# Every steady-state product of a two-layer graph kernel issued as two 64-column tiles of the TensorE array

## The chip, the cores and the metric

The kernel runs on one core of one Trainium2 chip. The metric is the device time of one execution in microseconds. Before the change it is 2427.78 us, the median of 6 runs (2426.64 to 2429.95).

## The reference

There are 128 graphs of 128 nodes with 512 features, and each has a 0/1 adjacency matrix. Layer 0 is graph attention with 8 heads of 64 features; layer 1 is a hypergraph convolution to 1024 features, a layer norm, and a second convolution back to 512. Each layer has a residual and a layer norm. Everything is fp32.

```python
# layer 0
feats = einsum('bnf,hfu->bhnu', X, W)                 # 512 -> 8 x 64
dense = leaky_relu(e_self[..., :, None] + e_neigh[..., None, :])
att = softmax(dense - 1e10 * (1 - A), axis=-1)
x = layernorm(x + relu(einsum('bhij,bhju->bhiu', att, feats) + b))
# layer 1
def hypergraph_conv(x, adj, W, b):
    H = (adj != 0); w = adj[:, 0, :]                   # weights: first row
    m = Be * einsum('nce,nch->neh', H, x @ W.T)        # Be = 1 / sum over nodes
    return Dn * einsum('nce,neh->nch', H, m) + b       # Dn = 1 / (H w)
h = layer_norm(relu(hypergraph_conv(x, adj, W1, b1)))  # 512 -> 1024
x = layernorm(x + hypergraph_conv(h, adj, W2, b2) + x) # 1024 -> 512
```

## The kernel before, in words

The graphs are taken in 64 pairs. All steps of a pair are functions that are recorded with a lag (in pairs) and a time; the list of all steps of all pairs is sorted by that time once, and in this order the instructions are given out (`todo`, at the end of the kernel). So each engine has one fixed order, in which up to five pairs are interleaved. The distance of two pairs in that order is `T = 38.6` units; only the order matters on the chip.

TensorE (PE) does per pair, with names of the PSUM tiles as the profile has them:

- `pz` (L808): the propagation of layer 0's output, 8 products of 128 stationary by 128 moving columns;
- `pd` (L435): the pair's propagator, 2 products of 128 by 128;
- `phX`, `phY`, `phW` (L843): the hidden convolution, 7 block products of 8 matmuls each, 128 by 128. The blocks are those of a seven-product (Strassen-like) scheme, with sums made by GpSimd and VectorE;
- `pq` (L1009): the last propagation, 2 products with 512 moving columns;
- `pfX`, `pfY`, `pfW` (L479, `rows_product`): layer 0's features, 7 block products of 2 matmuls each with 264 moving columns;
- `pyX`, `pyY`, `pyW` (L479 too): the second weights, 7 block products of 4 matmuls each with 257 or 256 moving columns;
- `pav` (L696, `attend_pair`): attention, 16 heads times two halves of the output rows.

The seven products accumulate in three banks, X, Y and W. ScalarE copies X after the first two of X's products (`copy`, L335) while PE is in the product between, and PE's next product into X waits for that copy.

`pav` alone is already given as column tiles: it writes output partitions 0 to 63 and 64 to 127 with two matmuls, each with 64 stationary columns and 65 moving ones. All other products have 128 stationary columns, the array's full width.

An fp32 matmul of the program becomes two pairs of a weight load (LDWEIGHTS) and a matmul (MATMUL) on PE; the profile counts those. The first two pairs and the last one have steps of their own (`plain_features` L516, `last_weigh` L1055, `last_output` L1091, transposes by PE in L388, L644, L976, L1062).

Of the kernel before, what the change touches and what calls it, by code (L numbers as in the profile page):

```python
# [20 lines left out]
def kernel(  # L21
# [45 lines left out]
    nc = tc.nc  # L67
    G, N, F = x.shape
    P = 128
# [3 lines left out]
    KF = F // P  # L73
    KH = DH // P
    HALF = 512
    QU = HALF // 2
# [12 lines left out]
    def bank(name):  # L89
        return psum.tile([P, HALF], F32, tag="bank", name=name)  # L90


    st = [{} for _ in range(PAIRS)]

# [212 lines left out]
    def step(lag, time, since=0, until=PAIRS):  # L307

        def keep(fn):
            steps.append((lag, time, fn.__name__, range(since, until), fn, ()))  # L310
            return fn
        return keep
# [117 lines left out]
    @step(1, 40.1)  # L430
    def propagator(p, s):

        s["pd"] = bank(f"pd_{p}")
        for g in range(2):
            nc.tensor.matmul(  # L435
                s["pd"][:, g * N:(g + 1) * N], s["hB"][:, g, :], s["hT"][:, g, :],
                start=True, stop=True,
            )

    @step(1, 40.2)  # L440
# [22 lines left out]
    def halves(t, n):  # L463
        return [[t[:, g, :n], t[:, g, n:]] for g in range(2)]
# [7 lines left out]
    def rows_product(s, i, a, sums, w, n, nk, extra, to, start):  # L472

        lhs = {1: a[0][0], 2: a[0][1], 3: sums[:, 3], 4: a[1][1], 5: sums[:, 0], 6: sums[:, 1],
               7: sums[:, 2]}[i]
        rhs = w[:, {1: 0, 2: 1, 3: 2, 4: 3, 5: 4, 6: 5, 7: 6}[i]]
        n += extra if i in (1, 2, 6) else 0
        for k in range(nk):
            nc.tensor.matmul(  # L479
                to[:, :n], lhs[:, k, :], rhs[:, k, :n], start=bool(start) and k == 0,  # L480
                stop=(k == nk - 1), skip_group_check=True,
            )

    FW = HH * UW
# [1 line left out]
    def feature(s, i, to, start):  # L486
        rows_product(s, i, halves(s["xT"], KF // 2), s["xS"],
                     w0_sb.rearrange("p b k h u -> p b k (h u)"), FW, KF // 2, 0, to, start)
# [316 lines left out]
    def propagate(p, s, g):  # L805
        t = s["pz", g] = bank(f"pz_{p}_{g}")
        for k in range(KF):
            nc.tensor.matmul(  # L808
                t[:, k * N:(k + 1) * N], s["y"][:, g, k * P:(k + 1) * P], s["R"][:, g, :],
                start=True, stop=True,  # L810
            )

    at(3, 0.0, propagate, 0)
    at(3, 0.9, propagate, 1)

    def z_evict(p, s, g):
# [19 lines left out]
    def hidden(s, i, to, start):  # L836
        w = w1_sb[:, {1: 0, 2: 1, 3: 6, 4: 2, 5: 3, 6: 4, 7: 5}[i]]
        b, t = halves(s["zT"], KF // 2), s["zS"]
        rhs = {1: b[0][0], 2: b[0][1], 3: b[1][1], 4: t[:, 3], 5: t[:, 0], 6: t[:, 1],
               7: t[:, 2]}[i]  # L840
        for m in range(KH // 2):
            for k in range(KF // 2):
                nc.tensor.matmul(  # L843
                    to[:, m * N:(m + 1) * N], w[:, k, m * P:(m + 1) * P], rhs[:, k, :],
                    start=bool(start) and m == 0 and k == 0, stop=(k == KF // 2 - 1),
                    skip_group_check=True,
                )

    chain("ph", 3, (2.0, 3.8, 5.6, 7.35, 9.1, 12.65, 14.4, 4.0, 5.95, 11.0), hidden,
          HALF)  # L850

# [60 lines left out]
    def weigh(s, i, to, start):  # L912
        rows_product(s, i, halves(s["h"], KH // 2), s["hS"], w2_sb, QU, KH // 2, 1, to, start)

    chain("py", 3, (21.0, 29.4, 27.7, 32.9, 31.2, 35.35, 37.1, 23.0, 29.6, 33.1), weigh,
          QU, 1, until=LAST)
# [89 lines left out]

    def output(p, s, g):
        s["pq", g] = bank(f"pq_{p}_{g}")
        nc.tensor.matmul(  # L1009
            s["pq", g], s["R"][:, g, :], s["y2"][:, g, :, :QU], start=True, stop=True  # L1010
        )

    at(4, 10.9, output, 0, until=LAST)
    at(4, 11.8, output, 1, until=LAST)

    def o_sum(p, s, g):
# [31 lines left out]
    def last_weigh(p, s, g, j, some=(0, 1)):  # L1048
        if some[0] == 0:
            s["py", g, j] = bank(f"py_{g}{j}")  # L1050
        t = s["py", g, j]
        n = QU + (j == 0)
        for i in some:
            for k in range(KH // 2):
                nc.tensor.matmul(  # L1055
                    t[:, :n], s["h"][:, g, i * KH // 2 + k, :], s["w2"][i][j][:, k, :n],
                    start=(i == 0 and k == 0), stop=(i == 1 and k == KH // 2 - 1),
                )

    def last_sum_squares(p, s, g):  # L1060
# [27 lines left out]
    def last_output(p, s, g, j):  # L1088
        if j == 0:
            s["pq", g] = bank(f"pq_{g}")  # L1090
        nc.tensor.matmul(  # L1091
            s["pq", g][:, j * QU:(j + 1) * QU], s["R"][:, g, :], s["y2"][:, g, j, :QU],
            start=True, stop=True,
        )

    def last_o_sum(p, s, g, j):
# [21 lines left out]
    for t, fn, *args in (  # L1118
        (8.0, last_weights),
        (24.2, last_weigh, 0, 0), (27.8, last_weigh, 0, 1), (31.3, last_sum_squares, 0),  # L1120
        (31.4, last_h_rstd, 0), (31.5, last_weigh, 1, 0), (32.5, last_scale, 0, 0),
        (32.6, last_scale, 0, 1), (34.9, last_sum_squares, 1), (35.0, last_h_rstd, 1),
        (35.1, last_output, 0, 0), (35.2, last_output, 0, 1), (35.3, last_weigh, 1, 1, (0,)),
        (35.5, last_o_sum, 0, 0), (35.6, last_scale, 1, 0), (36.0, last_o_sum, 0, 1),
        (36.5, last_o_rstd, 0), (37.0, last_output, 1, 0), (37.1, last_weigh, 1, 1, (1,)),
        (37.2, last_o_sum, 1, 0), (38.7, last_scale, 1, 1), (38.75, last_norm, 0),
        (38.9, last_output, 1, 1), (39.6, last_o_sum, 1, 1), (40.0, last_o_rstd, 1),
        (40.5, last_norm, 1),
    ):
        at(3, t, fn, *args, since=LAST)  # L1130
# [135 lines left out]
```

## Time and profile before

| what | value |
|---|---|
| median of 6 runs | 2427.78 us |
| the profiled execution's own time | 2427.62 us |
| its span, first to last instruction | 2425.8 us |
| mean granted TensorE clock | 0.997 |
| PE busy, share of the span | 2397.0 us, 99% |
| VectorE (DVE) / GpSimd (POOL) / ScalarE (ACT) busy | 80% / 74% / 63% |
| LDWEIGHTS and MATMUL on PE | 18273 of each |
| time from one pair to the next in the steady state | 37.05 us |

The busy times are unions of the instructions' recorded spans, and a matmul's recorded span reaches past the next one's start. So the mean of one (275 ns at 128 columns) is not what it costs; the distance from start to start is.

### The profile page before, as it was taken

What the parts mean: (1) busy time and instruction counts of PE and PEld (TensorE: products, weight loads), DVE (VectorE), ACT (ScalarE), POOL (GpSimd) and SP (SyncE); (2) the same over time, 40 slices, a digit from 0 to 9 for tenths busy, and PEclk for the clock granted to TensorE, in tenths of its full rate; (3) what the DMA queues carried; (4) which work ended last, traced back from release to release, by engine and by line L of the source; (5) the groups of instructions that cost most, each with busy time, mean ns of one, the idle gap of its engine ahead of it and who ended that gap; (6) DMA issues with size and microseconds to landing.
All of it is one profiled execution on the core that took longest, in us unless ns stands there. A gap on an engine that the chain in (4) does not pass through costs nothing.

```text
span 2425.8 us, 52771 instructions
## 1 busy us (share of the span) xinstructions
PE 2397.0 (99%) x18273; PEld 2139.6 (88%) x18273; DVE 1946.6 (80%) x4456; ACT 1516.8 (63%) x4481; POOL 1793.7 (74%) x2060
## 2 busy tenths in 40 slices
PE   7999999999999999999999999999999999999998
PEld 5888998998988988989989889889899898898897
DVE  7888878878878888888788788888887887888876
ACT  4665765756756657657567566576575675665763
POOL 5777777777777777777777777777777777777774
PEclk9999999999999999999999999999999999999999
DMA  6555545545455455454454554554545545545531
GB/s 186 140 140 153 146 132 151 146 135 151 141 144 148 140 153 145 133 154 142 137 147 148 141 148 142 151 147 132 155 143 134 153 141 146 145 140 153 147 111 53
DMA packets 432762, 345.30 MB, mean 142 GB/s; under 512 B 153176, under 2 KB 382064, under 8 KB 432496
## 3 DMA queue, kind: packets, MB, share of 16 engines
q1 hardware_dynamic: 429024, 337.46, 48.9%
q10 hardware_dynamic: 3472, 4.47, 0.6%
q8 instruction: 145, 2.38, 0.4%
q14 instruction: 121, 0.99, 0.2%
HBM read 239.08 MB, written 102.73 MB: 141 GB/s over the span
## 4 chain that ended last, share of the span: by engine, by line
PE 95%; DMA 2%; DVE 1%; POOL 1%; ACT 1%; issue 0%; SPq 0%; ACTq 0%; POOLq 0%; DVEq 0%
PE pyX L479 18%; PE phX L843 18%; PE pfX L479 9%; PE phW L843 9%; PE pyW L479 9%; PE pav L696 5%; PE pz L808 5%; PE pfW L479 5%; PE phY L843 4%; PE pyY L479 4%; PE pq L1009 4%; PE pfY L479 2%; PE pd L435 1%; DMA w<-in_w1t_dram 0%; PE py L1055 0%
## 5 line engine op out<-in xcount | busy, mean ns | idle before, releaser
L335 ACT COPY py<-pyX 128x257 f32<-128x257 f32 x189 | 70.9, 375 | 531.3 <-PE pyX L479 531.3
L843 PEld LDWEIGHTS phX<-zS,w_sb 128*128 128x128 f32 x3072 | 362.9, 192 | 34.3 <-issue 29.9
L843 PE MATMUL phX<-zS,w_sb 128*128 128x128 f32 x3072 | 374.5, 275 | 3.1 <-POOL xS L461 2.5
L896 POOL TENSOR_TENSOR sq<-sq 128x512 f32<-128x512 f32 (+2 forms) x384 | 323.3, 842 | 20.2
L582 POOL TENSOR_TENSOR nb<-nb,neg 128x512 f32<-128x512 f32 x256 | 318.2, 1276 | 7.8 <-DMA nb<-rd 7.8
L598 ACT ACTIVATE nb<-nb,ft 128x128 f32<-128x128 f32 x1020 | 318.0, 391 | 7.5 <-POOL nb L582 7.5
L758 POOL TENSOR_TENSOR rso<-veo,mhalf 128x2 f32<-128x2 f32 x63 | 44.1, 700 | 372.3 <-DVE veo L756 372.3
L612 ACT ACTIVATE nb<-nb,nm 128x128 f32<-128x128 f32 x1024 | 312.9, 391 | 2.0 <-DVE nm L604 1.9
L604 DVE TENSOR_REDUCE nm<-nb 128x4 f32<-128x512 f32 x256 | 172.6, 682 | 136.5 <-ACT nb L598 122.3
L873 ACT ACTIVATE h<-h,vecs 128x128 f32<-128x128 f32 x768 | 245.1, 392 | 46.5 <-DVE h L858 46.5
L479 PE MATMUL pyX<-w_sb,hS 128*128 128x257 f32 x1008 | 245.6, 385 | 0.0
L479 PE MATMUL pyX<-w_sb,h 128*128 128x257 f32 x1008 | 239.3, 379 | 0.5 <-ACT py L335 0.5
L479 PE MATMUL pyW<-w_sb,hS 128*128 128x256 f32 x1008 | 238.7, 379 | 1.0 <-DVE y L927 1.0
L479 PEld LDWEIGHTS pyX<-w_sb,h 128*128 128x128 f32 x1008 | 190.9, 190 | 29.0 <-ACT py L335 0.9
L479 PEld LDWEIGHTS pyW<-w_sb,hS 128*128 128x128 f32 x1008 | 190.6, 189 | 29.0 <-issue 1.4
L479 PEld LDWEIGHTS pyX<-w_sb,hS 128*128 128x128 f32 x1008 | 185.7, 189 | 28.7
L999 DVE SCALAR_TENSOR_TENSOR y<-y,rsh,bw_bc 128x512 f32<-128x512 f32 x126 | 148.0, 1213 | 32.6 <-POOL rsh L995 32.4
L633 DVE STREAM_TRANSPOSE eT<-eb 128x512 f32<-128x512 f32 x252 | 163.6, 687 | 1.1 <-DMA eb<-ed 1.1
L502 DVE TENSOR_TENSOR ft<-pf,pfW 128x264 f32<-128x264 f32 x124 | 53.3, 429 | 135.6 <-PE pfW L479 88.9
L884 ACT ACTIVATE sq<-h 128x512 f32<-128x512 f32 x256 | 160.5, 628 | 2.1
L461 POOL TENSOR_TENSOR hS<-h 128x512 f32<-128x512 f32 x126 | 159.0, 1282 | 1.9 <-ACT h L873 1.9
L733 POOL TENSOR_TENSOR y<-y,b_bc 128x512 f32<-128x512 f32 x128 | 160.0, 1271 | 0.0
(178 smaller groups left out, 5693.6 us busy)
## 6 DMA issues: line engine op xcount, KB each, us to landing
nb<-rd SPq DMA_DIRECT2D x127, 512.0 KB
ed<-nb SPq DMA_DIRECT2D x126, 512.0 KB
eb<-ed SPq DMA_DIRECT2D x504, 128.0 KB
x<-in_x_dram SPq DMA_DIRECT2D x64, 512.0 KB
out_dram<-o SPq DMA_DIRECT2D x63, 512.0 KB
xb<-in_x_dram SPq DMA_DIRECT2D x248, 128.0 KB
a<-in_adj_dram SPq DMA_DIRECT2D x64, 128.0 KB
w<-in_adj_dram SPq DMA_DIRECT2D x128, 64.0 KB
```

The source lines that it names most:

```text
L461: engine.tensor_tensor(t[:, i], in0, in1, op=op)
L479: nc.tensor.matmul(to[:, :n], lhs[:, k, :], rhs[:, k, :n], start=bool(start) and k == 0, stop=(k == nk - 1), skip_group_check=True,)
L582: nc.gpsimd.tensor_tensor(t, t, neg[:, :, None, :].to_broadcast([P, NB, HH, B]), op=ALU.add)
L598: nc.scalar.activation(t, t, AF.Prelu, bias=s["ft"][:, g, h, 0:1], alpha=SLOPE)
L604: nc.vector.tensor_reduce(s["nm"][:, g, hs], scores(p, s, g, hs).rearrange("p b h j -> p h b j"), AX.XY, ALU.max, negate=True,)
L612: nc.scalar.activation(t, t, AF.Exp, bias=s["nm"][:, g, h:h + 1])
L633: nc.vector.transpose(s["eT"][:, g, hs, :].rearrange("p h (b i) -> p h b i", b=NB), s["eb", g][:, :, hs, :].rearrange("p b h j -> p h b j"),)
L733: nc.gpsimd.tensor_tensor(s["y"][:, g, :], s["y"][:, g, :], b0_bc, op=ALU.add)
L843: nc.tensor.matmul(to[:, m * N:(m + 1) * N], w[:, k, m * P:(m + 1) * P], rhs[:, k, :], start=bool(start) and m == 0 and k == 0, stop=(k == ...
L873: nc.scalar.activation(dst[:, k, :], src[:, k, :], AF.Relu, bias=b1_sb[:, c:c + 1])
L884: nc.scalar.activation(s["sq"][:, g, q * KH // 2:(q + 1) * KH // 2, :], hid(s, g, q), AF.Square, scale=DH ** -0.5,)
L896: nc.gpsimd.tensor_tensor(t[:, :n, :], t[:, :n, :], t[:, n:2 * n, :], op=ALU.add)
```

## The change

A helper `columns` is added. It gives a product as two matmuls, one for the stationary columns 0 to 63 (output partitions 0 to 63) and one for columns 64 to 127 (output partitions 64 to 127), each with all the moving columns. The matmuls of `propagator`, `rows_product`, `propagate`, `hidden`, `output`, `last_weigh` and `last_output` go through it. `attend_pair` and `attend` were in this form already. `plain_features`, `prepare_output`, `prepare_output_spread` and the transposes are left with 128 columns.

```diff
+    def columns(to, lhs, rhs, start, stop):
+
+        for c in range(2):
+            rows = slice(c * P // 2, (c + 1) * P // 2)
+            nc.tensor.matmul(
+                to[rows], lhs[:, rows], rhs, start=start, stop=stop, skip_group_check=True
+            )
...
         for g in range(2):
-            nc.tensor.matmul(
-                s["pd"][:, g * N:(g + 1) * N], s["hB"][:, g, :], s["hT"][:, g, :],
-                start=True, stop=True,
+            columns(
+                s["pd"][:, g * N:(g + 1) * N], s["hB"][:, g, :], s["hT"][:, g, :], True, True
             )
...
         for k in range(nk):
-            nc.tensor.matmul(
-                to[:, :n], lhs[:, k, :], rhs[:, k, :n], start=bool(start) and k == 0,
-                stop=(k == nk - 1), skip_group_check=True,
+            columns(
+                to[:, :n], lhs[:, k, :], rhs[:, k, :n], bool(start) and k == 0, k == nk - 1
             )
...
         for k in range(KF):
-            nc.tensor.matmul(
+            columns(
                 t[:, k * N:(k + 1) * N], s["y"][:, g, k * P:(k + 1) * P], s["R"][:, g, :],
-                start=True, stop=True,
+                True, True,
             )
...
             for k in range(KF // 2):
-                nc.tensor.matmul(
+                columns(
                     to[:, m * N:(m + 1) * N], w[:, k, m * P:(m + 1) * P], rhs[:, k, :],
-                    start=bool(start) and m == 0 and k == 0, stop=(k == KF // 2 - 1),
-                    skip_group_check=True,
+                    bool(start) and m == 0 and k == 0, k == KF // 2 - 1,
                 )
...
-        nc.tensor.matmul(
-            s["pq", g], s["R"][:, g, :], s["y2"][:, g, :, :QU], start=True, stop=True
-        )
+        columns(s["pq", g], s["R"][:, g, :], s["y2"][:, g, :, :QU], True, True)
...
             for k in range(KH // 2):
-                nc.tensor.matmul(
+                columns(
                     t[:, :n], s["h"][:, g, i * KH // 2 + k, :], s["w2"][i][j][:, k, :n],
-                    start=(i == 0 and k == 0), stop=(i == 1 and k == KH // 2 - 1),
+                    i == 0 and k == 0, i == 1 and k == KH // 2 - 1,
                 )
...
-        nc.tensor.matmul(
-            s["pq", g][:, j * QU:(j + 1) * QU], s["R"][:, g, :], s["y2"][:, g, j, :QU],
-            start=True, stop=True,
+        columns(
+            s["pq", g][:, j * QU:(j + 1) * QU], s["R"][:, g, :], s["y2"][:, g, j, :QU], True, True
         )
```

## The prediction

> **What bounds the kernel now.** I read the busy table first, then the chain that ended last, then PE's waits, and last PE's order of time over one pair.
>
> ```profile
> span 2425.8 us, 52771 instructions
> PE 2397.0 (99%) x18273; PEld 2139.6 (88%) x18273; DVE 1946.6 (80%) x4456; ACT 1516.8 (63%) x4481; POOL 1793.7 (74%) x2060
> PE 95%; DMA 2%; DVE 1%; POOL 1%; ACT 1%; issue 0%; SPq 0%; ACTq 0%; POOLq 0%; DVEq 0%
> ```
>
> ```profile
> PE px L388 <- DMA x<-in_x_dram: 9.5, 1, 9.5
> PE pz L808 <- ACT y L785: 6.8, 1, 6.8
> PE phX L843 <- POOL xS L461: 2.5, 1, 2.5
> PE pyW L479 <- DVE y L927: 1.0, 1, 1.0
> ```
>
> PE is 99% busy and carries 95% of the chain. Its waits for others sum to some 23 us, single ones, all in the first 90 us or the last pair. In the 62 steady pairs PE waits for nobody, so the change is worth what it makes of PE's own stream. This is one stretch of it, in order of time:
>
> ```profile
> 1112.39 1.05 PE L479 MATMUL pfX<-w_sb,xS 128*128 128x264 f32 x4
> ...
> 1117.69 1.05 PE L479 MATMUL pfW<-w_sb,xS 128*128 128x264 f32 x4
> 1118.67 2.09 PE L696 MATMUL pav<-ft,eT 128*64 128x65 f32 x64
> 1120.69 2.01 PE L479 MATMUL pyX<-w_sb,hS 128*128 128x257 f32 x8
> 1122.53 1.90 PE L479 MATMUL pyY<-w_sb,h 128*128 128x257 f32 x8
> 1124.27 1.89 PE L479 MATMUL pyX<-w_sb,hS 128*128 128x256 f32 x8
> ...
> 1131.19 1.95 PE L808 MATMUL pz<-R,y 128*128 128x128 f32 x16
> ...
> 1137.01 1.95 PE L843 MATMUL phX<-zS,w_sb 128*128 128x128 f32 x16
> ...
> 1142.37 1.89 PE L1009 MATMUL pq<-y,R 128*128 128x512 f32 x4
> 1144.09 1.95 PE L843 MATMUL phX<-zS,w_sb 128*128 128x128 f32 x16
> ```
>
> From start to start, a full-width matmul takes 430 ns at 512 moving columns (1.72 us for 4), 216.3 at 256 (from 1124.27 to 1131.19 there are 32), 222.5 at 264 (other pf groups are 0.89 us for 4) and 111.7 at 128 (1137.01 to 1142.37, 48). The line through 256 and 512 is 2.5 ns + 0.835 ns a column. It gives 222.9 at 264, as measured, but 109.4 at 128: there each matmul has 2.3 ns over the line. At 128 a weight load of 128 columns stands against a stream of 128, so the two are tied; with longer streams the load is hidden.
>
> Attention's own rate, from the count of its matmuls in growing windows (the x after PE's busy time):
>
> ```profile
> 1118.90:1119.00 0.10, 0.10 (x10) 1.00 1.12 282
> 1118.90:1120.40 1.50, 1.50 (x58) 1.00 0.61 109
> ```
>
> 48 more in 1.40 us: 29.2 ns each, 58.3 ns for two. Two streams of 65 columns one after the other would be 2 x 56.8 = 113.6 by the line. So the two column tiles run side by side, loads included, at 1.5 ns over the line; here too load (64) and stream (65) are tied.
>
> **The change part by part.**
>
> *The mode changes go.* pav is entered and left by groups of another width. The last pf group should be followed at 1117.69 + 0.89 = 1118.58; pav starts at 1118.67: 0.09 us. 32 times 58.3 ns is 1.87 us, so pav's streams would be over at 1120.54, but pyX starts at 1120.69: 0.15. pyX then takes 1.84 us for what the next 257 group does in 1.74: 0.10, a first weight load that nothing covers. Sum 0.34 us. The view of pav's tile says the same from the weight loads' side:
>
> ```profile
> L696 PEld LDWEIGHTS pav<-ft,eT x3968: 132/138/140, 77.9 to 2343.3; 128*64 128x64 f32 x199
>   issue: 21.7, 63
> ```
>
> That is 0.345 us each. 62 steady pairs: 62 x 0.345 = 21.4 us gone, since nothing of another width is left in them.
>
> *Twice the matmuls, half the width.* 7018 more matmuls of the program are 14036 more weight loads and as many matmuls (18273 to 32309). If the two of each product run side by side as pav's do, a product keeps its time; what is open is the excess over the line per slot of two. Two rows bound it: 1.5 ns (pav's, tied) and 0 (the untied 264). In the changed kernel a 64-column load stands against streams of 128 and more, so I take the untied row, 0. Then the 128-column products (7168 + 1024 + 256 = 8448 matmuls in L843, L808, L435) fall from 111.7 to 109.4: 8448 x 2.3 = 19.4 us gone, and the 256 to 512 ones stay. With 1.5 ns everywhere the 8448 gain only 0.8 ns (6.8 us) and the other 88 slots of a pair lose 1.5 ns (88 x 1.5 x 63 = 8.3 us): 1.5 us lost.
>
> *New mode changes.* The full-width transposes among products of the last two pairs (L976 once, L1062 twice) now stand alone in their width: 3 x 0.34 = 1.0 us, less one visit of pav in the last pair, 0.34: 0.7 us lost. The start keeps both kinds side by side.
>
> *Waits.* The order on all other engines is unchanged. PE's first matmul of a product carries the wait, and the second tile's load now stands behind two loads and two matmuls of the first tile; at pav's 29.2 ns for a load and a matmul that is 58 ns, when PE arrives with nothing queued. The tight places are the products after ScalarE's copy of X (ScalarE's own order of time, same stretch):
>
> ```profile
> 1111.80 0.36 ACT L335 COPY pf<-pfX 128x264 f32<-128x264 f32 x1
> ```
>
> The copy ends at 1112.16 and pfX goes on at 1112.39 (first line of the stretch above), 0.23 us later, without a gap on PE. That covers 58 ns; the two other tight ones (the second pf copy, and zT before phX) look alike. Bounds: 0 and 3 x 58 ns x 62 = 10.8 us; I take 2, since all three are covered now. If the cover were gone, PE would stand until ScalarE's copy is through. The added waits of PE on its own semaphore (at phW, pq and pav) are for products at least 35 slots back: nothing, covered by those slots.
>
> *Instruction fetch.* Its queue takes 145 packets, 2.38 MB, 0.4% of 16 engines: about 1 us each, one per 17 us. It becomes some 256, one per 9.5 us. Hidden unless a packet is 8 us late.
>
> *Others.* DVE has 30.2 us of work in a pair's 37.05, POOL 27.9, ACT 23.6; a pair of 36.4 us still covers them.
>
> Sum against the profiled execution's own 2427.62 us (0.2 us off the median): -21.4 - 19.4 + 0.7 + 2 = -38.1, 2389.5. I say 2390.
>
> [...]
>
> **The rivals.**
>
> *Pav's excess stays* at 1.5 ns in every slot. For: it is the only column row. Against: it is tied, like the 128 row, and the untied rows have none. -21.4 + 1.5 + 2.7 = -17: 2410.
>
> *Two streams share a read path* (the other side). Each tile reads the moving operand for itself. If pav's 58.3 ns for 65 columns is all rate, 0.897 ns a column, then 128 columns take 114.8 (+3.1 x 8448 = 26 us), 256 or 257 230.1 (+13.2 x 56 x 63 = 47), 264 236.8 (+14.3 x 28 x 62 = 25), 512 459 (+29 x 4 x 63 = 7): 105 - 21.4 = +84, 2511. It decides from a rate 0.0085 ns a column (1%) above full width on, where 40700 columns a pair eat the 0.345 us. Against: pav moves two streams and two loads at once within 3% of the line.
>
> *Issue does not keep up beyond a burst.* pav is a burst of 128 loads and matmuls that can stand in a queue beforehand; the longest stretch of 128-wide products shows 111.7 ns for 2 instructions only. If 55.9 ns an instruction were the limit, four would need 223 ns: 8448 x 111.7 = +944 us. From 27.9 ns an instruction on, it costs. pav's 14.6 ns speaks against it, and a queue of 128 would have to hide it.
>
> *The tiles don't run side by side* outside pav (the change doesn't do what it says): PE's stream doubles, +2200 us. pav's 58.3 ns excludes it nearly.
>
> *Others become the bound.* The tight copies eat the gain: 0.67 us less a pair against 0.23 us of distance at the tightest. Where all three floors bind, 10.8 us come back and more behind them: 2400 to 2425.
>
> **How the numbers follow.** Untied, 0.50 (2378 to 2402); pav's excess, 0.25 (2403 to 2418); others take it back, 0.08; shared read path 0.11 (2435 to 2511); issue or serial tiles 0.04; nothing moves 0.02. A measurement can tell 0.2%, 4.9 us, from no change. Faster: 0.50 + 0.25 + 0.06 = 0.81; same: 0.02 + 0.02 + 0.02 from a weak read path = 0.06; slower: 0.13. The range 2378 to 2432 leaves out the slower cases and a twentieth below.
>
> **What would show it.** Right: no "issue" idle at pav, pyX after pav 1.74 us; ph groups of 32 at 1.75 us instead of 1.786; py and pf groups unchanged at 1.73 and 0.89; PE waits still single; a pair in 36.4 us. Wrong: groups of 256 and more longer than now (read path); 128 groups much longer and others not (issue); new waits of PE on ACT's L335 copies in every pair. The forecast fails most easily by the step that takes pav's short streams as proof for long ones.

## The result, and the profile after

The changed kernel takes 2434.33 us (median of 18 runs, 2431.51 to 2435.55); the kernel before, timed beside it, 2427.91 us (38 runs). The ratio is 1.0024, 95% interval 1.0018 to 1.0030. It is slower by 0.24%, where 2390 us and a range of 2378 to 2432 were forecast.

The profiled execution of the changed kernel took 2429.98 us. Its page, with the span, the busy times, and the chain that ended last by engine:

```profile
span 2428.2 us, 80910 instructions
PE 2388.5 (98%) x32309; PEld 1985.2 (82%) x32309; DVE 1941.9 (80%) x4456; ACT 1511.0 (62%) x4481; POOL 1796.9 (74%) x2060
...
POOL 42%; DVE 28%; PE 12%; DMA 10%; issue 4%; ACT 1%; SPq 1%; POOLq 0%; DVEq 0%; ACTq 0%
```

The busy shares have hardly moved, but the chain has: PE held 95% of it and now holds 12%; POOL and DVE hold 70%. PE's order of time over one pair, from a pf group to the same group of the next pair:

```profile
1110.65 1.06 PE L97 MATMUL pfX<-w_sb,xT 128*64 128x264 f32 x8
1111.54 1.06 PE L97 MATMUL pfY<-w_sb,xT 128*64 128x264 f32 x8
1112.72 1.11 PE L97 MATMUL pfX<-w_sb,xS 128*64 128x264 f32 x8
...
1118.93 2.07 PE L702 MATMUL pav<-ft,eT 128*64 128x65 f32 x64
1120.80 1.94 PE L97 MATMUL pyX<-w_sb,hS 128*64 128x257 f32 x16
1122.54 1.94 PE L97 MATMUL pyY<-w_sb,h 128*64 128x257 f32 x16
...
1127.74 1.93 PE L97 MATMUL pyX<-w_sb,h 128*64 128x256 f32 x16
1129.56 1.95 PE L97 MATMUL pyW<-w_sb,hS 128*64 128x256 f32 x16
...
1133.06 0.64 PE L97 MATMUL pd<-hT,hB 128*64 128x128 f32 x8
1133.76 1.97 PE L97 MATMUL phX<-zT,w_sb 128*64 128x128 f32 x32
...
1137.30 1.92 PE L97 MATMUL phX<-zS,w_sb 128*64 128x128 f32 x32
...
1140.80 1.92 PE L97 MATMUL phX<-zS,w_sb 128*64 128x128 f32 x32
...
1147.78 1.06 PE L97 MATMUL pfX<-w_sb,xT 128*64 128x264 f32 x8
```

Every group is as long as forecast. From start to start pav takes 1.87 us (1118.93 to 1120.80) and the pyX after it 1.74, where it took 1.84. The 128-column groups take 1.75 us (1137.30 to 1140.80 is two), where they took 1.786. The 256 and 264 groups keep 1.73 and 0.89. With each group at the time it has where nothing disturbs it, a pair is 7 x 0.89 + 3 x 1.74 + 4 x 1.73 + 1.87 + 1.745 + 0.435 + 7 x 1.745 + 1.72 = 36.4 us.

The pair on show takes 37.13 (1110.65 to 1147.78). PE now stands at three places in it: 1.18 us instead of 0.89 before the second product into pf's X bank, 0.70 instead of 0.44 from pd to phX, 1.82 instead of 1.73 before the last pyW. That is 0.29 + 0.26 + 0.09 = 0.64 us; the rest is 0.02 to 0.05 in groups beside them. Over the steady pairs the medians of these three stands are 0.29, 0.24 and 0.08 us. The median distance of two pairs, from the trace, is 37.10 us after and 37.04 before.

The view of PE's waits still has only single ones, the same as before, since a group's recorded span (1.06 us at pfY) reaches over most of a stand (the next group starts 1.18 us after it). So the sign "PE waits still single" could not tell right from wrong here. The weight loads' rows show the stands (us in total, times, longest). First the kernel before, then after:

```profile
PEld phX L843 <- issue: 29.9, 124, 0.3
PEld pav L696 <- issue: 21.4, 62, 0.3
PEld pfX L479 <- POOL rso L758: 3.5, 19, 0.4
PEld pyW L479 <- issue: 1.4, 1, 1.4
```

```profile
PEld pfX L97 <- POOL rso L764: 33.7, 60, 0.6
PEld phX L97 <- issue: 26.0, 70, 0.5
PEld pyW L97 <- issue: 18.7, 60, 0.3
PEld phX L97 <- ACT zT L826: 18.1, 61, 0.3
```

The row of pav's mode change is gone, as forecast. Three others, of some 60 times each, one a pair, stand in its place: pfX, pyW and the wait for zT. (The first row names POOL's `rso`, which ends at 1112.59; in the program the product waits for ScalarE's copy of pfX, the row below, which ends at 1112.58, and PE goes on at 1112.72.)

```profile
1112.22 0.36 ACT L343 COPY pf<-pfX 128x264 f32<-128x264 f32 x1
```

What holds the pair at 37.1 us is the chain that ended last. Here it is in order of time, from one `rso` (POOL's power for the output norm) to the next:

```profile
1111.89 0.70 POOL rso L764
1112.59 1.25 POOL sq L901
...
1115.31 2.48 POOL hS L468 x2
...
1123.10 0.46 DVE sq L947
...
1129.17 0.70 POOL rsa L764
1129.87 4.96 POOL nb L588 x4
1134.83 0.70 POOL zS L837
...
1138.26 0.72 POOL rsh L1000
1139.01 2.09 DVE y L1004 x2
...
1143.69 0.39 DVE hB L434 x2
...
1148.77 0.18 DVE veo L762
1149.02 0.70 POOL rso L764
```

This is a closed ring of one pair's length. POOL goes from `rso` through the sums of squares and of h; DVE takes those sums over (`sum_blocks`, L947) and goes on to attention's norm; POOL takes that (`rsa`) and adds the mask, sums zT and gives `rsh`; DVE scales y (L1004) and goes on through the outputs to `veo`, which releases the next pair's `rso`. Different pairs are in the four legs, but each engine's fixed order ties them into a ring. POOL and DVE are 74% and 80% busy, yet one of them is always at work for the ring, and its idle time is the other's leg. The ring was there before, with the same handovers. POOL's `rso` of two neighbouring pairs, before:

```profile
1111.48 0.70 POOL L758 TENSOR_TENSOR rso<-veo,mhalf 128x2 f32<-128x2 f32 x1 [5.87 <-DVE veo L756]
...
1148.55 0.70 POOL L758 TENSOR_TENSOR rso<-veo,mhalf 128x2 f32<-128x2 f32 x1 [5.87 <-DVE veo L756]
```

After, the same wait of POOL is 5.87 us as well. So before, two things took 37.04 us a pair at once: PE's own stream, and this ring. Medians over the steady pairs, from the traces (ns; a leg runs from the start of its first instruction to the start of the next leg's; lines are those of the kernel after, and `sums_in`, L948, is the second instruction of `sum_blocks`, 0.48 us behind L947):

| kernel | POOL rso to DVE sums_in, L948 | to POOL rsa | to DVE L1004 | to the next rso | sum |
|---|---|---|---|---|---|
| before | 11664 | 5580 | 9803 | 9998 | 37046 |
| after | 11688 | 5586 | 9826 | 10006 | 37105 |

### The profile page after: what moved, and what is told of

It reads as the page before. It is cut to its first block, busy times and chain, and to the rows that moved or that the text cites. A ratio compares the mean times of both kernels' runs of the same rounds, so it can differ in the third digit from the quotient of the medians.

```text
span 2428.2 us, 80910 instructions
## 1 busy us (share of the span) xinstructions
PE 2388.5 (98%) x32309; PEld 1985.2 (82%) x32309; DVE 1941.9 (80%) x4456; ACT 1511.0 (62%) x4481; POOL 1796.9 (74%) x2060
## 3 DMA queue, kind: packets, MB, share of 16 engines
q8 instruction: 255, 4.18, 0.7%
## 4 chain that ended last, share of the span: by engine, by line
POOL 42%; DVE 28%; PE 12%; DMA 10%; issue 4%; ACT 1%; SPq 1%; POOLq 0%; DVEq 0%; ACTq 0%
POOL nb L588 10%; POOL hS L468 10%; POOL sq L901 9%; POOL zS L837 6%; DVE y L1004 5%; DMA sd<-sr 4%; DVE o L802 4%; DMA nb<-rd 3%; DVE statso L756 3%; DVE o L1021 3%; PE phX L97 2%; PE pfX L97 2%; DVE xT L384 2%; DVE nm L610 2%; POOL rsa L764 2%
## 5 line engine op out<-in xcount | busy, mean ns | idle before, releaser
L97 PEld LDWEIGHTS phX<-zS,w_sb 128*64 128x64 f32 x6144 | 345.4, 137 | 38.1 <-issue 26.0
L97 PE MATMUL phX<-zS,w_sb 128*64 128x128 f32 x6144 | 368.2, 273 | 2.7 <-POOL xS L468 2.2
L97 PE MATMUL pyW<-w_sb,hS 128*64 128x256 f32 x2016 | 244.3, 381 | 1.5 <-DVE y L932 1.5
L97 PE MATMUL pyX<-w_sb,h 128*64 128x257 f32 x2016 | 243.5, 379 | 0.5 <-ACT py L343 0.5
L97 PE MATMUL pyX<-w_sb,hS 128*64 128x257 f32 x2016 | 243.6, 379 | 0.0
L97 PEld LDWEIGHTS pyW<-w_sb,hS 128*64 128x64 f32 x2016 | 164.9, 136 | 61.4 <-issue 18.7
L97 PEld LDWEIGHTS pyX<-w_sb,h 128*64 128x64 f32 x2016 | 171.8, 136 | 48.0 <-ACT py L343 0.9
L97 PEld LDWEIGHTS pyX<-w_sb,hS 128*64 128x64 f32 x2016 | 165.3, 137 | 40.7
L1004 DVE SCALAR_TENSOR_TENSOR y<-y,rsh,bw_bc 128x512 f32<-128x512 f32 x126 | 147.8, 1212 | 35.3 <-POOL rsh L1000 35.1
```

The lines of the kernel that those rows point to most:

```text
L97: nc.tensor.matmul(to[rows], lhs[:, rows], rhs, start=start, stop=stop, skip_group_check=True)
L1004: nc.vector.scalar_tensor_tensor(t, t, s["rs", "h"][:, g:g + 1], bw_bc.rearrange("p (j c) -> p j c", j=2), op0=ALU.mult, op1=ALU.add,)
```

## The experiments

Theory: PE's stream became 0.69 us a pair shorter, as forecast, and the ring, which was already as long as PE's old stream, sets the pair. Rival: the column form itself delays PE (its queue, its waits, the copies), and ScalarE's copies alone take the gain back.

### e1: the changed kernel, one pair of DVE instructions moved out of the ring's longest DVE leg

```diff
-    @step(1, 10.8)
+    @step(1, 1.65)
     def scale_edges(p, s):        # hB, L434
...
-        ("edges", 0): 14.46, ("edges", 2): 119.2,
+        ("edges", 0): 14.46, ("edges", 2): 119.2, ("scale_edges", 2): 126.6,
```

The last line sets the step's place for one pair at the start.

> The changed kernel with scale_edges (two DVE instructions, 0.40 us a pair) moved out of the stretch in which DVE never stands still to a place where it waits for ACT and a DMA. Theory: a ring of POOL and DVE work with no idle time in it has taken over at 37.11 us a pair; 0.40 us less in it gives 36.7 us a pair, 62 x 0.4 = 25 us less, 2409 us. Rival, PE's own stream costs more in column tiles (lost in the restarts at pfX, phX and pyW): what DVE does elsewhere changes nothing, 2434. Rival, ScalarE's copies are too slow by themselves for the faster PE: 2430 to 2434.

Measured: 2422.33 us (2417.75 to 2425.27) against 2430.09 for the kernel before, timed beside it as in all that follow, ratio 0.9966, interval 0.9954 to 0.9979. The DVE leg fell from 10006 to 9615 ns and the typical pair from 37.10 to 36.74. Nothing on PE was touched, and PE's stands shrank by about what was taken out of the ring: in the median the one at pfX is gone (890 ns from pfY to pfX, 1184 in the changed kernel), the one at pyW is 0.04 us, and the one at phX stays. 15 of 59 pairs were over 0.2 us longer than the typical one, 11 us in all; e9 shows what goes with such pairs.

### e2: the same, and the node weights moved too

The lines that are added to e1's edit:

```diff
-    @step(0, 11.0)
+    @step(0, 35.7)
     def nodes(p, s):
...
-    @step(0, 17.0)
+    @step(0, 35.71)
     def write_nodes(p, s):
```

> The changed kernel with scale_edges and nodes (about 2 us of DVE a pair together) moved out of that stretch. Theory: the ring falls to about 35.2 us a pair, PE binds again at 36.4 us, 2389 us, with PE's restarts at pfX, phX and pyW gone. Rival, PE's stream itself is dearer in column tiles: 2434. Rival, the copies: 2430 to 2434.

Measured: 2426.60 us (2419.84 to 2430.19), ratio 0.9984 (0.9975 to 0.9993). A miss: it loses half of what e1 gains. The instructions of `nodes`, now under POOL's mask additions, grew, and so did L426 of `edges` behind them. DVE's order of time in e2, then POOL's:

```profile
1124.02 1.12 DVE L364 TENSOR_SCALAR dn<-dd 128x2 f32<-128x2 f32 x1
...
1125.38 0.99 DVE L366 SCALAR_TENSOR_TENSOR dn<-dd,dn 128x2 f32<-128x2 f32 x1
...
1127.60 1.25 DVE L426 TENSOR_SCALAR deg<-deg 128x2 f32<-128x2 f32 x1
```

```profile
1123.71 5.11 POOL L588 TENSOR_TENSOR nb<-nb,neg 128x512 f32<-128x512 f32 x4
```

In the changed kernel L364 takes 0.17 us, L366 0.16 and L426 0.79 (medians). Here L364 ends at 1125.14, L366 at 1126.37 and L426 at 1128.85; POOL's four additions, 1.28 us each, end at about 1124.99, 1126.27, 1127.54 and 1128.82. Each of the three DVE instructions ends within 0.2 us of the end of one of POOL's. DVE's maxima (`nm`) and so ScalarE come later by this, and PE stands at another place:

```profile
1138.61 1.97 PE L97 MATMUL phX<-zS,w_sb 128*64 128x128 f32 x32 [0.30 <-ACT ph L343]
```

This stand is 0.34 us in the median of all pairs (2064 ns from pq to phX, 1720 in the changed kernel), and in the median the three stands of the changed kernel are gone. So the ring no longer holds e2 (POOL has 2% of its chain). PE's groups, 36.36 us, and this stand make 36.70 of a typical pair's 36.76, which is no shorter than e1's. What e2 loses against e1 lies, in the traces, in the long pairs: 23 of 59 are over 0.2 us longer than the typical one, 17.8 us in all. The profiled execution is the slowest of e2's 11, so that sum is no typical one.

### e3: both moves on the kernel before

The edit is that of e2, on the kernel before.

```diff
-    @step(0, 11.0)
+    @step(0, 35.7)
     def nodes(p, s):
...
-    @step(0, 17.0)
+    @step(0, 35.71)
     def write_nodes(p, s):
...
-    @step(1, 10.8)
+    @step(1, 1.65)
     def scale_edges(p, s):
```

> The kernel before with the same two moves. Theory: full-width PE needs 37.05 us a pair and bound it already, so 2427 with 3 us either way. Rival, the ring of POOL and DVE bound the kernel before too and PE only followed: 2400 to 2420.

Measured: 2428.08 us against 2430.09, ratio 0.9993 (0.9984 to 1.0002). Unchanged: with full-width products PE's own stream keeps the pair at 37.04 us.

### e4: the kernel before, the ring made longer by a known instruction

```diff
+    scr = const.tile([P, 2 * N], F32, name="scr")
+    nc.gpsimd.memset(scr, 0.0)
+
+    @step(3, 17.15)
+    def longer(p, s):
+        nc.gpsimd.tensor_tensor(scr, scr, scr, op=ALU.subtract)
```

> The kernel before with one more POOL instruction a pair (128x256 of fp32 on a scratch tile, about 0.70 us as zS has it) between squares of the first graph, where POOL has no idle time. Theory: the ring had almost no slack before the change either, so nearly all of it is paid: 62 x 0.70 = 43 us, 2471, less its slack (at most 0.1 us a pair, 6 us). Rival, POOL's 26% of idle time is slack of the kernel before: 2428 to 2433.

Measured: 2463.34 us against 2430.09, ratio 1.0136 (1.0122 to 1.0150). The added instruction in POOL's order of time in e4:

```profile
1130.23 0.80 POOL L907 TENSOR_TENSOR scr<-scr 128x256 f32<-128x256 f32 x1
```

POOL's leg grew from 11664 to 12243 ns, 0.58 us, and the pair from 37.04 to 37.62, 0.58 us. The record of the instruction is longer, 0.80 us, but part of it falls into short pauses between the sums of squares: from the start of the sum before it to that of the first `hS` behind it is 1.92 us (median), 1.36 without it, so it adds 0.56. POOL is idle 26% of the time before the change, and none of that took up the 0.58 us: the other three legs kept their length within 0.01 us. This shows the second bound in the kernel before, with PE's products untouched. (It doesn't show by itself that PE had no room either; e11 and e12 do.) Two rows of the weight loads in e4:

```profile
PEld pyW L479 <- issue: 26.6, 60, 0.5
PEld phX L843 <- ACT zT L820: 11.0, 61, 0.2
```

With full-width products and a longer ring, PE stands at two of the three places of the changed kernel, once a pair: 1.96 us instead of 1.73 before the last pyW, 0.60 instead of 0.45 from pd to phX (medians). So a ring that is longer than PE's stream makes such stands without any column tile.

### e5, e7: the changed kernel, a transpose of DVE moved

```diff
-    at(0, 28.95, x_transpose, 1, since=2)
+    at(0, 36.0, x_transpose, 1, since=2)      # e7: at(1, 1.65, ...)
```

> The changed kernel with the second transpose of x (one DVE instruction, 1.1 us) moved from the stretch between sum_blocks and the layer norm of layer 0 to the place where DVE stands 1.7 us waiting for ScalarE's leaky. Theory: this stretch is part of the ring, which falls from 37.1 to 36.0 us a pair, so PE binds at 36.4 us, 62 x 0.7 = 43 us less than the changed kernel: 2390 us (up to 2405 if transfers come late in some pairs). Rival, the column tiles cost PE what they save: 2434.

> As the run before with the column tiles, but with the transpose at DVE's other idle place, 2.1 us waiting for the sums' transfer. Theory: the same gain, 2390 to 2405; if the new place delays ScalarE's copies of phX, which stand behind DVE's maxima, some 0.2 us a pair come back, 2405 to 2415. Rival: 2434.

Measured: e5 2440.14 us against 2428.89, ratio 1.0039 (1.0026 to 1.0051); e7 2436.87, 1.0032 (1.0020 to 1.0044). Both miss. The transpose (1.0 us) stands in the ring's chain, but the leg did not get shorter without it. In e5 the next instruction, the residual, starts at once and lasts until POOL is through with its second addition (DVE's row, then POOL's):

```profile
1499.77 1.74 DVE L748 SCALAR_TENSOR_TENSOR y<-y,x 128x512 f32<-128x512 f32 x1
```

```profile
1498.46 2.50 POOL L739 TENSOR_TENSOR y<-y,b_bc 128x512 f32<-128x512 f32 x2
```

POOL's additions end at 1500.96 and the residual at 1501.51, 0.55 us later. In the kernel before it ran behind the transpose:

```profile
1123.75 1.07 DVE L376 STREAM_TRANSPOSE xT<-xb 128x512 f32<-128x512 f32 x1
1124.74 0.93 DVE L742 SCALAR_TENSOR_TENSOR y<-y,x 128x512 f32<-128x512 f32 x1
...
1126.83 0.69 DVE L742 SCALAR_TENSOR_TENSOR y<-y,x 128x512 f32<-128x512 f32 x1
```

There POOL's additions (1122.61 for 2.51) ended at 1125.12 and the residual at 1125.67, again 0.55 later; one that has no POOL instruction beside it takes 0.69. So the ring has a second way through this leg, by POOL's additions, and the transpose only filled the time of it. Where the chain is drawn through an instruction, taking the instruction away need not shorten it.

### e6: the same move on the kernel before

```diff
-    at(0, 28.95, x_transpose, 1, since=2)
+    at(0, 36.0, x_transpose, 1, since=2)
```

> The kernel before with the same move. Theory: full-width PE alone needs 37.04 us a pair, so no change, 2425 to 2430. Rival, the ring alone bound it: about 2400.

Measured: 2429.61 us against 2428.89, ratio 1.0000 (0.9992 to 1.0009): unchanged. Since the move doesn't shorten the ring (e5), this is no test of PE's bound.

### e8: e5 with part of the products at full width again

The edit is e5's, and the products of `propagator`, `propagate`, `hidden` and `output` are single matmuls of 128 stationary columns again, as in this one; `rows_product` stays in columns.

```diff
-            columns(
+            nc.tensor.matmul(
                 t[:, k * N:(k + 1) * N], s["y"][:, g, k * P:(k + 1) * P], s["R"][:, g, :],
-                True, True,
+                start=True, stop=True,
             )
```

> The changed kernel with the moved transpose, but with the 128- and 512-column products (hidden, propagate, propagator, output) back at full width, so that a pair still has one run of column tiles (pf, pav, py) and one of full width. Theory: the mode is still changed twice a pair (0.34 us) and the 128-column matmuls keep 111.7 ns, so PE needs 37.05 us a pair, 2427. Rival, only attention's short products pay for a change of mode: 36.7 us, 2406.

Measured: 2432.89 us against 2428.89, ratio 1.0015 (1.0006 to 1.0023), a typical pair of 37.09. It doesn't tell the theories apart. By the prices that the trace gave, PE's stream is 36.36 + 0.32 (the 128-column products' tie) + 0.34 (one change of mode a pair) = 37.02; the ring is 37.085 in this trace; and the chain that ended last is PE's for 95%.

### e9: the changed kernel, hB taken off DVE

```diff
-    @step(1, 10.8)
+    @step(1, 24.6)
     def scale_edges(p, s):
...
-            nc.vector.tensor_scalar(
-                s["hB"][:, g, :], s["hT"][:, g, :], s["be"][:, g:g + 1], None, op0=ALU.mult
+            nc.scalar.activation(
+                s["hB"][:, g, :], s["hT"][:, g, :], AF.Identity, scale=s["be"][:, g:g + 1]
             )
```

> The changed kernel with scale_edges taken off DVE altogether: ScalarE makes the two products, at a place where it stands 4 us without work. Theory: the ring of POOL and DVE is 0.40 us shorter and nothing else is hit, so a pair takes 36.7 us, 62 x 0.4 = 25 us less than the changed kernel: 2409 us, to 2420 if transfers come late in some pairs, as they did when scale_edges was moved on DVE. Rival, the gain of that run came from elsewhere: 2434.

Measured: 2420.64 us (2416.85 to 2423.89) against 2428.95, ratio 0.9967 (0.9954 to 0.9979). e1 and e9 are alike within their intervals, and both are faster than both kernels. The ring is 36733 ns (legs 11704, 5585, 9826, 9615). PE's order of time at pfX, where the changed kernel stood 0.29 us a pair:

```profile
1142.28 1.06 PE L97 MATMUL pfX<-w_sb,xT 128*64 128x264 f32 x8
1143.16 1.06 PE L97 MATMUL pfY<-w_sb,xT 128*64 128x264 f32 x8
1144.06 1.06 PE L97 MATMUL pfX<-w_sb,xS 128*64 128x264 f32 x8
```

0.90 us to the next group, no stand, with the same column form on PE. So the rival falls: it isn't the form that delays PE there. ScalarE's copies alone don't either: ScalarE has more to do here (1548.5 us busy against 1511.0), and the stand is gone. What keeps the typical pair from 36.4 is the ring still. Besides, 13 of 59 pairs are over 0.2 us longer, 10 us in all, and transfers come late in most of these: counted from `rso` to `rso` 14 are long, and in 11 of them DVE waits over 0.3 us for a transfer before eT or xT, 25.5 us in all. DVE's waits for attention's transposed weights, in the changed kernel and in e9 (us, times, longest):

```profile
DVE eT L639 <- DMA eb<-ed: 7.0, 11, 1.2
```

```profile
DVE eT L639 <- DMA eb<-ed: 31.5, 30, 2.6
```

### e10, e11: POOL's additions of squares left out, after and before

```diff
-        nc.gpsimd.tensor_tensor(t[:, :n, :], t[:, :n, :], t[:, n:2 * n, :], op=ALU.add)
```

> The changed kernel without POOL's squares: the additions that sum the squares over the eight blocks are left out (so the second norm's variance is wrong); POOL has 5.2 us a pair less to do and all of it lies in the ring. Theory: the ring is out of the way, PE binds with its shorter stream, 36.4 us a pair, 2390 us; up to 2405 if the next ring (scores through memory) is close. Rival, PE's stream in column tiles needs 37.1 us: 2434.

> The kernel before without the same additions (same part left out). Theory: full-width PE needs 37.04 us a pair whatever POOL does: 2425 to 2430. Rival, the ring alone set the time before too: 2400 or less.

Measured: after without them 2419.83 us against 2428.95, ratio 0.9967 (0.9957 to 0.9977); before without them 2429.34, 1.0001 (0.9992 to 1.0010). The two runs separate the bounds: 4.7 us of POOL's work a pair ((1796.9 - 1498.4) / 64, six instructions) is worth nothing before the change and 0.4 us a pair after it (37.10 to 36.70 in the median). It is half a miss too, for 2390 us was expected. The undisturbed pairs stopped at 36.62 us, since the next limit is close behind. PE's order of time in e10:

```profile
1141.85 1.06 PE L97 MATMUL pfY<-w_sb,xT 128*64 128x264 f32 x8
1143.03 1.11 PE L97 MATMUL pfX<-w_sb,xS 128*64 128x264 f32 x8
```

PE still takes 1.18 us there, as in the changed kernel. And 22 of 59 pairs were longer than the median by 11.3 us in all, with longer waits of DVE for transfers (17.5 us for eT, 7.0 in the changed kernel).

### e12: e9's move on the kernel before

```diff
-    @step(1, 10.8)
+    @step(1, 24.6)
     def scale_edges(p, s):        # and nc.vector.tensor_scalar -> nc.scalar.activation, as in e9
```

> The kernel before with the same single move as the best version (scale_edges taken off VectorE and given to ScalarE, 24.6 units into the pair). Theory (two bounds at one height: PE's own stream and the ring of POOL and VectorE, each 37.04 us a pair): the ring gets 0.39 us shorter, PE stays at 37.04, so a typical pair stays at 37.04 to 37.06 and the time within 0.1% of before, 2427 to 2430. Rival (the move itself is what made the best version faster, by taking work off VectorE, whatever form the products have): the pair falls here too, by some 0.3 us, and the time by 0.3%, to about 2421. What it tells: whether the 8 us of the best version belong to the column tiles together with the move, or to the move alone.

Measured: 2426.93 us against 2428.98, ratio 0.9996 (0.9987 to 1.0005). Its chain that ended last, by engine:

```profile
PE 97%; DVE 1%; DMA 1%; issue 0%; POOL 0%; ACT 0%; SPq 0%; POOLq 0%; DVEq 0%; ACTq 0%
```

The pair is 37.04 as before. The ring's last leg fell from 9998 to 9703 ns and its second from 5580 to 5326, and its first grew from 11664 to 12212: POOL and DVE now wait for the rest of the kernel, which PE paces. So the 8 us of e9 are neither the move's nor the column tiles' alone. Each of the two shortens one of two equal bounds, and only both together shorten the pair.

## Why the prediction was wrong

The step that failed is this one: "*Others.* DVE has 30.2 us of work in a pair's 37.05, POOL 27.9, ACT 23.6; a pair of 36.4 us still covers them." It compares sums of busy time with the pair. The sums were right (29.96, 27.94 and 23.54 us in the ring on show after), but the room they leave is no slack: POOL's longest idle time, 5.87 us a pair, is DVE's leg of the ring. The ring was 37.046 us in the trace of before, and e4 showed that it had no slack that could be measured. With it went the term "Waits", taken as 2 us and bounded at 10.8, since that bound counted only the 58 ns of a longer queue at three places and not the copies coming late against a shorter pair. All of the 0.69 us, some 43 us over 62 pairs, came back as stands of PE: at pfX and at phX after zT, two of the places that the term names, and at the last pyW, which waits for DVE (its addition of the pyW before ends at 1129.41, and PE goes on at 1129.56). The 0.23 us between copy and pfX, which the term counts as cover, were not all cover: where PE stands for the copy, it goes on 0.14 us behind the copy's end (1112.58 to 1112.72). The sign that the prediction gave for this, new waits of PE on ScalarE's copies in every pair, is what the weight loads' row of pfX shows.

The rival "Others become the bound" had the right heading, with a chance of 0.08 and a price of 2400 to 2425, but not the ring: the mechanism it named was ScalarE's tight copies, sized (0.23 us of distance at the tightest) as if they came at a fixed time. They come when the ring lets them, and all of the gain was taken back, so even this rival's price was too low.

What was right, by the steps:

- The mode changes cost what was read from the trace (0.345 us each), and they went: no "issue" idle at a steady pav, pyX after it at 1.74 us.
- The two tiles run side by side at all lengths of this kernel (1.72 us for 4 slots of 512 columns, 0.89 for 4 of 264, 1.73 for 8 of 256, as at full width), and the excess is that of the untied row: 1.745 us for 16 slots of 128 is 109.1 ns a slot, against 109.4 by the line. The rivals of a shared read path, of issue and of serial tiles are out, as is pav's excess in every slot.
- Instruction fetch: 255 packets and 4.18 MB against the 256 forecast, and no wait is put down to it.

So PE's share of the forecast, 36.4 us a pair, was met within 0.05 us, as a sum of groups where nothing disturbs them. No kernel ran steadily at it; the shortest of e9's steady pairs is 36.42 us from pd to pd, behind one of 37.90. In the changed kernel the pair was not PE's any more.

That it is slower and not the same goes with the ring's own growth: 37105 against 37046 ns, 0.06 us a pair, 3.7 us over 62 pairs. The profiled spans differ by 2.4 us (from the first `rso` to the last by 3.5, so what lies outside was 1.1 us shorter), the medians by 6.4; unlike before, the profiled execution of the changed kernel lies below all its others, and what makes those 1.5 us or more longer was not seen. The growth lies in POOL's legs (+24 and +23 ns of the 61). POOL's mask addition has a median of 1272 to 1278 ns in the six traces with full-width products and of 1277 to 1281 in the eight with column tiles. The two ranges touch. That the column tiles cause it is argued from this, not shown; how they would was not tried.

PE was the busiest engine before, with 99% (its weight loads 88%) against DVE's 80%. Yet 0.69 us a pair off PE alone gained nothing, hB's 0.39 us off DVE alone (e12) nothing that can be measured, and both together 8 us.

## What to carry to other kernels

Before pricing a gain on the engine that is busiest, follow the others' handovers round one period: when every idle time of POOL ends at DVE and the reverse, and the legs add up to the period, the two are a second bound, whatever their busy shares. The cheap proof is to lengthen the ring by one instruction; if the period grows by all that it adds to its engine's leg, and the other legs stay, there is no slack, and a faster bottleneck gains nothing until that ring is shortened too. Test such a shortening on both kernels: only the pair of results (e9 with e12, e10 with e11) tells which bound it touched.

## What the runs showed of the hardware that was not expected

- Some DVE instructions took longer beside POOL's. A 128x2 one (L364) takes 0.17 us in the median of the changed kernel and 1.12 in e2's row; hB takes 274 ns in the median of the changed kernel, 756 in e1 and 772 in e2; the residual 0.69 us alone and 1.74 in e5's row. Those on show end within 0.2 us of the end of a POOL instruction (e2) or 0.55 us after it (the residual). What holds them until then no run shows. So in e2 and e5 moving DVE's work in time had a price that its busy time before did not show.
- The kernels with a shorter pair had more long pairs: 13 to 22 of 59 were longer than the median by over 0.2 us in e1, e9 and e10, 10 to 11 us in all, where before there is one. In most of e9's, DVE waits for a transfer; its wait for eT is 31.5 us there, 7.0 in the changed kernel. Why these transfers come late was not tried.
